# Three edits to an attention and convolution kernel: another queue for the last inverses, earlier reloads of the angle tables, and a new place for the sums of four heads

## The chip, the cores and the metric

The kernel runs on one core of one Trainium2 chip. A core has a matrix engine (TensorE, "PE" in the profile, with its weight loads listed apart as "PEld"), a vector engine (VectorE, "DVE"), an engine for activation functions (ScalarE, "ACT"), a general engine (GpSimd, "POOL") and one that only issues transfers (SyncE, "SP"). Each works through its own list of instructions in order and waits on semaphores for the others. Transfers are issued by SP or by POOL here, and all of them are carried out by the core's 16 DMA engines. The metric is the device time of one execution in microseconds.

## What is computed

Two layers are applied to a float32 input of shape (4, 1024, 32, 32), that is 4 images of 1024 channels and 1024 positions. The first layer is attention over the positions with 16 heads of 64 channels, the second is a bottleneck of three convolutions with normalization over the batch. Cut to what matters:

```python
# layer 1 of 2, per image: x is (N=1024 positions, C=1024 channels)
qkv = x @ w_qkv.T + b_qkv                 # q, k, v: 16 heads of 64
q, k = rope(q), rope(k)                   # pairs (2i, 2i+1) turned by cos and sin tables
q = q * rsqrt(mean(q * q) + eps) * q_w    # over all 1024 channels; k likewise
attn = softmax(q @ k.T / 8)               # per head
out = rmsnorm((attn @ v) @ w_proj.T) * norm_out_w + x
# layer 2 of 2
h = relu(bn(conv1x1(out)));  h = relu(bn(conv3x3(h)));  h = bn(conv1x1(h))
return relu(out + softplus(residual_scale) * h)
```

## The kernel before

The four images (the code calls them batches, b = 0 to 3) go through the attention layer one after the other; the convolutions follow. Channels lie on the 128 partitions, in eight tiles (NT = 8), and positions along the free axis in two halves of 512 (NCH = 2). For every image the stages are: projection to q, projection to k, projection to v, the scores and contexts of the heads, and the output projection.

**Projections.** They are matrix products by a Strassen-like scheme in two levels (`project2`; q and k of image 0 take one level, `project`). There are seven outer operand blocks k, with seven inner products each. One inner product of `project2` is a group of eight matmul instructions of 256 columns, since a float32 matmul is made of two. Each inner product needs a weight chunk of 256 KB, which SP loads into a ring of eight buffers (`chunk`); `start(k + 1)` queues the loads of the next block between the third and the fifth product of this one. Sums of weights were prepared in DRAM during image 0 (`wdf`, `wd2f`), by steps that share VectorE and SP with the attention of image 0. VectorE makes the sums of the right operands (L450 to L454) and adds partial results (L506, L525).

**The order of the work.** The lists of TensorE, POOL, VectorE and ScalarE are written out by hand, in the order in which the code emits; SP's list is ordered by the compiler's planner, which estimates times. The code keeps a clock of its own while it emits, `pace["at"]`, in units of one large product (two inner products of `project2` are one unit): `product_done` advances it, `after(n, step)` puts a step n units later, and `waiting` holds steps that go out when there is room on VectorE. While the last block of the v projection is emitted, `waiting` is held (`pace["hold"]`). `rest(leave)` empties the lists until `leave` steps remain.

**Rotation** (`rope`, L705 to L740). q and k are turned tile by tile: VectorE multiplies the tile by the sine table (into another buffer) and by the cosine table (in place), and POOL issues two accumulating transfers that add the first product with neighbouring rows exchanged (L727, "the exchange"). Before this, `tables` (L715) multiplies both tables in place by the inverse root mean square of this image. So the tables must be loaded anew before the next rotation: after the last tile POOL issues three loads (L176 twice for sines, L177 for cosines), and `then` holds the next rotation back until 3.7 units after the point at which the last tile was emitted.

**Scores and contexts** (`attention`). It is called for each half c of the query positions, and goes through eight pairs of heads (hp). For each of eight blocks t of key positions TensorE makes a score tile of both heads (`sc`, L787), ScalarE takes the exponential (L794), and VectorE adds it into the running denominators `d_` (L798 and L800). After the eight score tiles come the contexts (`cx`, L808). In the first half (c = 0) denominators are folded to eight heads at a time, by transfers of POOL (`halve`, `sum_of_eight`). In the second half (c = 1, `fold` is None), after each odd pair, four matmuls with a block of ones (`dn`, L841) sum the denominators of four heads over the partitions, directly behind the contexts. The three kinds of matmul use the array in different shapes: the records list them as 64*128 (scores), 128*64 (contexts) and 128*32 (denominators). At the start of the next pair ScalarE copies `dn` out (L891), SP stores it and loads it back in another layout, VectorE takes the reciprocal, and SP spreads the inverses over the partitions (`spread`, L910). `mean_of_v` then scales the contexts on VectorE (L764) and adds the bias of v on POOL (L765).

**The last four heads of an image** have no next pair. Their `dn` follows the last contexts, and their `inverses` step is emitted shortly after the start of the output projection: VectorE takes the reciprocal of all 512 columns (L893), SP stores them (L894) and spreads them by eight transfers (L910). `mean_of_v` for them is emitted three units after the start of the projection, and the sums of the second part of its right operands (L281 to L284) four units after. In the same stretch SP issues the weights of the projection and the loads of the next image (of the last: of what the convolution reads back, L1107).

Of the kernel before, what the change touches and what calls it, by code (L numbers as in the profile page):

```python
# [11 lines left out]
F32 = mybir.dt.float32  # L12
# [6 lines left out]
P = 128  # L19
B, C, H, W = 4, 1024, 32, 32  # L20
N = H * W
NT = C // P
HD = 64
NHP = C // (2 * HD)
CH = 512
# [38 lines left out]
QH = P // 4  # L64
# [21 lines left out]
def program(ctx, tc, x, wblk, w2, w3, vecs, cos, sin, out, bad):  # L86


    nc = tc.nc
# [9 lines left out]
    ones = const.tile([P, P], F32, name="ones")  # L99
# [16 lines left out]
    def col(name, i=0):  # L116
        return vec[:, COL[name] + i : COL[name] + i + 1]
# [35 lines left out]
    dens = dram.tile([P, CH], F32, name=f"dens{u}")  # L153
# [4 lines left out]
    with tc.tile_pool(name=f"st{u}", bufs=2) as st, ExitStack() as s:  # L158
# [6 lines left out]
        acc = s.enter_context(tc.tile_pool(name=f"acc{u}", bufs=2))  # L165
# [4 lines left out]
        cosT = tp.tile([P, N], F32, tag="cos", name="cosT")  # L170
        sinT = tp.tile([P, N], F32, tag="sin", name="sinT")

        def load_tables(queue):
            for i in range(2):

                queue.dma_start(sinT[i::2, :], sin[1 - i :: 2, :])  # L176
            queue.dma_start(cosT, cos)  # L177

        ident = None
# [5 lines left out]
        half = [slice(c * CH, (c + 1) * CH) for c in range(NCH)]  # L185
# [17 lines left out]
        def bank(kind, name):  # L203
            pool, shape = psum[kind]
            return pool.tile(shape, F32, tag=kind, name=name)
# [43 lines left out]
        pace = {"at": 0, "room": 0.0, "hold": False, "tables": 0.0}  # L249
# [459 lines left out]
        def rope(b, dst, total, eps, scale, w, tag, biased=True):  # L709

            def tables():
                for t in (sinT, cosT):
                    nc.vector.tensor_tensor(t, t, total, ALU.mult)  # L715

            def turn(f):
                k, other = dst[:, f, :], big_temp(f"{tag}s_{b}_{f}")
                for i, (t, table) in enumerate(((other, sinT), (k, cosT))):
                    if w is not None:  # L720
                        nc.vector.scalar_tensor_tensor(t, k, w[i][:, f : f + 1], table, ALU.mult, ALU.mult)
                    elif biased:
                        nc.vector.tensor_tensor(t, k, table, ALU.mult)
                    else:
                        nc.vector.scalar_tensor_tensor(t, k, col("bq", f), table, ALU.add, ALU.mult)
                for i in range(2):
                    nc.gpsimd.dma_start(dst[i::2, f, :], other[1 - i :: 2, :], accum_op=ALU.add)  # L727
                if f == NT - 1 and (b, tag) != (B - 1, "k"):
                    load_tables(nc.gpsimd)
                    pace["tables"] = pace["at"] + 3.7  # L730

            def then():
                if pace["at"] < pace["tables"]:
                    after(pace["tables"] - pace["at"], then)
                    return
                waiting.append((4 * TT, tables))
                for f in range(NT):
                    waiting.append((4 * TT, lambda f=f: turn(f)))

            inverse_rms(total, eps, scale, f"{tag}_{b}", then)  # L740
# [26 lines left out]
        def attention(b, c, q_all, k_all, v, probs_, late, ready, extra, slow, steps_in_all, load_parts, fold):  # L767


            at = half[c]  # L770
            sums_ = []
            for hp in range(NHP):
                n = f"{b}_{c}_{hp}"
                if late:
                    late.pop(0)()
                rows = shifts(q_all, k_all, n, hp, c) if bad is None else None
                probs = []
                if fold and hp % 2 == 0:
                    d_ = fold[hp // 4][:, hp % 4 // 2 * 2 : hp % 4 // 2 * 2 + 2, :]
                else:  # L780
                    d_ = acc.tile([P, 2, CH], F32, tag="tot", name=f"den_{n}")
                for t in range(N // P):
                    p = probs_[:, t]
                    sc = bank("sc", f"sc_{n}_{t}")
                    for j in range(2):
                        d = slice(j * HD, (j + 1) * HD)
                        nc.tensor.matmul(  # L787
                            sc[:, j], k_all[d, hp, t * P : (t + 1) * P], q_all[d, hp, at],
                            start=True, stop=bad is not None,
                        )  # L790
                    if bad is None:
                        for j in range(2):
                            nc.tensor.matmul(sc[:, j], ones[0:1, :], rows[j], start=False, stop=True)
                    nc.scalar.activation(p, sc, AF.Exp)  # L794
                    if t == 3:
                        load_parts()
                    if t == 1:
                        nc.vector.tensor_tensor(d_, probs[0], p, ALU.add)  # L798
                    elif t > 1:
                        nc.vector.tensor_tensor(d_, d_, p, ALU.add)  # L800
                    probs.append(p)
                if eights and eights[0][0] <= c * NHP + hp:
                    eights.pop(0)[1]()
                o = bank("cx", f"cx_{n}")
                for t in range(N // P):
                    for j in range(2):
                        h0 = (2 * hp + j) * HD
                        nc.tensor.matmul(  # L808
                            o[j * HD : (j + 1) * HD, :], v[:, t, h0 : h0 + HD], probs[t][:, j],
                            start=(t == 0), stop=(t == N // P - 1),  # L810
                        )

                nc.scalar.copy(q_all[:, hp, at], o)  # L813
                sums_.append(d_)
                if hp % 2 == 1:
                    for r in ready:
                        mean_of_v(q_all, *r)
                    ready.clear()
                if fold:
                    halve(hp, d_, fold[hp // 4][:, hp % 4 // 2 * 2 : hp % 4 // 2 * 2 + 2, :])  # L820
                    if hp % 4 == 3:
                        eights.append((hp + 2, lambda n=n, hp=hp: sum_of_eight(b, n, hp, fold[hp // 4], ready)))
                if half_done and half_done[0][0] <= c * NHP + hp:
                    half_done.pop(0)[1]()
                if slow:
                    slow.pop(0)()

                if waiting:
                    next_waiting()
                slots = NCH * NHP - 1  # L830
                if extra and steps_in_all == 0 and hp > 0:
                    extra.pop(0)()
                for _ in range(len(extra) - -(-steps_in_all * max(slots - 1 - c * NHP - hp, 0) // slots) if steps_in_all else 0):
                    extra.pop(0)()
                if hp % 2 == 0 or fold:
                    continue
                dn = bank("dn", f"dn_{n}")
                for i, d_ in enumerate(sums_):
                    for j in range(2):
                        q = slice((2 * i + j) * QH, (2 * i + j + 1) * QH)  # L840
                        nc.tensor.matmul(dn[q, :], ones[:, :QH], d_[:, j], start=True, stop=True)  # L841
                sums_ = []
                late.append(lambda *a, n=n, hp=hp, dn=dn: inverses(b, c, hp, n, dn, ready))

        half_done, eights = [], []
        low, high = slice(0, P // 2), slice(P // 2, P)
# [38 lines left out]
        def inverses(b, c, hp, n, dn, ready):  # L885


            r = temp(f"rec_{n}")
            k = 2 * ((b * NCH + c) * NHP + hp - 1)

            nc.scalar.copy(r, dn)  # L891
            if (c, hp) == (NCH - 1, NHP - 1):
                nc.vector.reciprocal(r, r)  # L893
                nc.sync.dma_start(dens[k : k + 4, :], r[::QH, :])  # L894
                spread(c, hp, n, ready, [r[q * QH : (q + 1) * QH, :] for q in range(4)])
                return
            few, rows = to_few(n, k, 4, r[::QH, :])

            def invert():
                nc.vector.reciprocal(few, few)  # L900
                nc.sync.dma_start(rows, few)
                spread(c, hp, n, ready, [dens[k + q, :].partition_broadcast(QH) for q in range(4)])

            half_done.append((0, invert))

        def spread(c, hp, n, ready, rows):
            w = big_temp(f"inv_{n}")
            for i in range(2):
                for j in range(4):
                    nc.sync.dma_start(w[j * QH : (j + 1) * QH, half[i]], rows[2 * i + j // 2])  # L910
                ready.append((c, hp - 1 + i, w[:, half[i]]))

        def o_norm(b, total, ys):
# [245 lines left out]
        load_x(0, 0, range(NH, NT))  # L1159
        w1 += [block(WQ, g, 1, f"q_0_{g}_1") for g in range(NG)]  # L1160
        load_x(0, 1)
        load_tables(nc.sync)
        queue_sums(ts[0], xs[0])
        room = v_room("rq_0")
        for b in range(B):
# [500 lines left out]
```

## Time and profile before

| | |
|---|---|
| median of 3 runs | 2677.93 us (2675.83 to 2679.2) |
| profiled execution | 2679.37 us, its span on the core 2677.6 us |
| granted TensorE clock, mean | 0.997 |
| VectorE busy | 2112.0 us (79%) |
| ScalarE busy | 1113.8 us (42%) |
| POOL busy | 434.3 us (16%) |
| DMA queue of SP (hardware) | 328.75 MB, 39.3% of 16 engines' span |
| DMA queue of POOL (software) | 131.45 MB, 20.7% |
| scores and contexts, image 0 / 1 / 2 / 3 begin at | 287.8 / 864.6 / 1442.1 / 2017.7 us |
| output projection, image 0 / 1 / 2 / 3 begins at | 522.4 / 1096 / 1674 / 2249.4 us |

The page gives the busy time of each engine and, for each group of instructions, what ended the idle time before it. A wait that is put down to one engine ended with that engine's instruction. The timeline lists instructions by start and length in microseconds from the start of the span, merges neighbours of one kind (x16 means sixteen), and writes in brackets the idle time of the engine before and who ended it. An "SPq" line is an issue: the transfer itself lands later.

### The profile page before, as it was taken

The page shows a single profiled execution, that of the slowest core. Times are in us where ns is not written, and L with a number is a line of the kernel's source. Part 1 is how long each engine was busy: PE and PEld are TensorE (multiplying, and loading weights), DVE is VectorE, ACT ScalarE, POOL GpSimd, SP SyncE. Part 2 cuts the span into 40 slices and gives each one's busy share as a digit, 9 for nine tenths or more (in the row PEclk, how much of TensorE's full clock was granted, in tenths as well). Part 3 has the DMA queues.
Part 4 walks back from the last instruction along what each step waited for, and adds up shares of the span by engine and source line. Part 5 has one row for each costly group of instructions (what it writes and reads, how often), then busy time and mean ns, then how long its engine had stood idle before and what let it go on. Part 6 is the DMA issues. An engine that isn't in the chain of part 4 may idle for free. (4 is left out here: it accounts for less than half of the span.)

```text
span 2677.6 us, 32431 instructions
## 1 busy us (share of the span) xinstructions
PE 2646.0 (99%) x11322; PEld 1652.9 (62%) x11322; DVE 2112.0 (79%) x2536; ACT 1113.8 (42%) x1551; POOL 434.3 (16%) x501
## 2 busy tenths in 40 slices
PE   9999999999999999999999999999999999999997
PEld 4448533488888333688886333888884335846843
DVE  5668989997888766888878767887978679877987
ACT  2222455423442555333343555233525554312266
POOL 2542202100111222100111222100111222010000
PEclk9999999999999999999999999999999999999999
DMA  7887787767667551556775441665774443593165
GB/s 279 289 253 216 223 239 239 239 201 221 201 186 204 96 92 34 166 156 218 194 199 131 92 79 30 213 204 175 192 212 87 80 103 105 163 279 115 64 232 208
DMA packets 261387, 462.37 MB, mean 173 GB/s; under 512 B 34528, under 2 KB 127248, under 8 KB 261216
## 3 DMA queue, kind: packets, MB, share of 16 engines
q1 hardware_dynamic: 222048, 328.75, 39.3%
q0 software_dynamic: 39168, 131.45, 20.7%
q8 instruction: 93, 1.52, 0.2%
q14 instruction: 78, 0.64, 0.1%
HBM read 327.43 MB, written 97.01 MB: 159 GB/s over the span
## 5 line engine op out<-in xcount | busy, mean ns | idle before, releaser
L794 ACT ACTIVATE p<-sc 128x1024 f32<-128x1024 f32 x512 | 476.7, 1047 | 26.5 <-PE sc L787 25.8
L787 PE MATMUL sc<-q,k 64*128 64x512 f32 x2048 | 457.7, 596 | 0.0
L800 DVE TENSOR_TENSOR den<-den,p 128x1024 f32<-128x1024 f32 x288 | 356.1, 1236 | 30.4 <-DVE den L800 0.5
L787 PEld LDWEIGHTS sc<-q,k 64*128 64x128 f32 x2048 | 189.9, 186 | 265.2 <-issue 121.7
L808 PE MATMUL cx<-p,to 128*64 128x512 f32 x1536 | 340.2, 595 | 0.0
L808 PEld LDWEIGHTS cx<-p,to 128*64 128x64 f32 x1536 | 106.0, 137 | 228.8 <-issue 228.8
L480 PE MATMUL p_v<-w_v,x 128*128 128x256 f32 x928 | 211.7, 382 | 2.8 <-DVE x L451 2.8
L485 PE MATMUL p_y<-q,w_y 128*128 128x256 f32 x928 | 209.8, 379 | 0.0
L765 POOL TENSOR_SCALAR q<-q,vec 128x512 f32<-128x512 f32 x64 | 128.2, 2014 | 436.3 <-DVE q L764 436.3
L480 PEld LDWEIGHTS p_v<-w_v,x 128*128 128x128 f32 x928 | 177.3, 191 | 28.6 <-DVE x L451 3.9
L485 PEld LDWEIGHTS p_y<-q,w_y 128*128 128x128 f32 x928 | 176.0, 190 | 27.1 <-issue 3.4
L813 ACT COPY q<-cx 128x512 f32<-128x512 f32 x64 | 37.6, 587 | 360.7 <-PE cx L808 360.7
L798 DVE TENSOR_TENSOR den<-p 128x1024 f32<-128x1024 f32 x48 | 59.7, 1245 | 117.5 <-ACT p L794 117.5
L485 PE MATMUL p_q<-to,w_q 128*128 128x256 f32 x672 | 152.2, 379 | 0.0
L485 PE MATMUL p_k<-to,w_k 128*128 128x256 f32 x672 | 152.2, 379 | 0.0
L485 PEld LDWEIGHTS p_q<-to,w_q 128*128 128x128 f32 x672 | 127.4, 190 | 18.4 <-issue 1.2
L485 PEld LDWEIGHTS p_k<-to,w_k 128*128 128x128 f32 x672 | 127.4, 190 | 18.4 <-issue 1.2
L800 DVE TENSOR_TENSOR den_T<-den_T,p 128x1024 f32<-128x1024 f32 x96 | 117.6, 1226 | 10.4 <-ACT p L794 0.5
L808 PE MATMUL cx<-p,rq 128*64 128x512 f32 x512 | 113.4, 595 | 0.0
L1570 PE MATMUL c<-h,w 128*128 128x512 f32 x256 | 110.3, 592 | 0.5 <-ACT h L1473 0.5
L485 PE MATMUL p_y<-to,w_y 128*128 128x256 f32 x384 | 91.3, 383 | 5.8 <-DMA w_y<-wdf 5.8
L480 PE MATMUL p_v<-w_v,t 128*128 128x256 f32 x384 | 90.2, 379 | 0.9 <-DMA w_v<-wdf 0.8
(488 smaller groups left out, 4205.0 us busy)
## 6 DMA issues: line engine op xcount, KB each, us to landing
w_v<-wd2f SPq DMA_DIRECT2D x112, 256.0 KB, 3.3
w_y<-wd2f SPq DMA_DIRECT2D x112, 256.0 KB, 2.8
w_q<-wd2f SPq DMA_DIRECT2D x84, 256.0 KB, 2.7
w_k<-wd2f SPq DMA_DIRECT2D x84, 256.0 KB, 2.7
wd2f<-w_pre SPq DMA_DIRECT2D x68, 256.0 KB, 2.7
x<-in_x_dram SPq DMA_DIRECT2D x64, 256.0 KB, 5.0
q<-qs POOLq DMA_DIRECT2D x64, 256.0 KB, 5.5
k<-ks POOLq DMA_DIRECT2D x64, 256.0 KB, 4.4
```

Source lines behind the costliest of these rows:

```text
L480: nc.tensor.matmul(o[:, q].rearrange("p (g f) -> p g f", g=2), r[:, i, q * P : (q + 1) * P], wt[:, :, i, :], skip_group_check=True, **at,)
L485: nc.tensor.matmul(o[:, q], wt[:, q, i, :], r[:, i, :], skip_group_check=True, **at)
L765: nc.gpsimd.tensor_scalar(cx, cx, col("bv", hp), None, ALU.add)
L787: nc.tensor.matmul(sc[:, j], k_all[d, hp, t * P : (t + 1) * P], q_all[d, hp, at], start=True, stop=bad is not None,)
L794: nc.scalar.activation(p, sc, AF.Exp)
L798: nc.vector.tensor_tensor(d_, probs[0], p, ALU.add)
L800: nc.vector.tensor_tensor(d_, d_, p, ALU.add)
L808: nc.tensor.matmul(o[j * HD : (j + 1) * HD, :], v[:, t, h0 : h0 + HD], probs[t][:, j], start=(t == 0), stop=(t == N // P - 1),)
L813: nc.scalar.copy(q_all[:, hp, at], o)
L1570: nc.tensor.matmul(os[i], w3t[k][f // NH][:, f % NH, :], h2[b, k][:, half[c]], start=(k == 0), stop=(k == NPT - 1),)
```

## The change

It has three parts. First, `load_tables` is split into the sines and the cosines, and each is issued right behind the product that used the old table of the last tile, ahead of that tile's two exchange transfers; the next rotation is held back 5 units instead of 3.7. Second, in the second half of the attention the four `dn` matmuls of a group are no longer emitted behind the contexts of the odd pair, but in the next pair behind its second score tile, together with the copy and the store that follow them; the running denominators of that next pair get their buffer after this. The last group of an image stays where it was. Third, for this last group the store and the eight spreads are issued by POOL's queue instead of SP's.

```diff
-        def load_tables(queue):
+        def load_sines(queue):
             for i in range(2):
                 queue.dma_start(sinT[i::2, :], sin[1 - i :: 2, :])
+
+        def load_cosines(queue):
             queue.dma_start(cosT, cos)
...
                         nc.vector.scalar_tensor_tensor(t, k, col("bq", f), table, ALU.add, ALU.mult)
+                    if f == NT - 1 and (b, tag) != (B - 1, "k"):
+                        (load_sines, load_cosines)[i](nc.gpsimd)
                 for i in range(2):
                     nc.gpsimd.dma_start(dst[i::2, f, :], other[1 - i :: 2, :], accum_op=ALU.add)
-                if f == NT - 1 and (b, tag) != (B - 1, "k"):
-                    load_tables(nc.gpsimd)
-                    pace["tables"] = pace["at"] + 3.7
+                if f == NT - 1:
+                    pace["tables"] = pace["at"] + 5
...
-            sums_ = []
+            sums_, fours = [], []
...
-                if fold and hp % 2 == 0:
-                    d_ = fold[hp // 4][:, hp % 4 // 2 * 2 : hp % 4 // 2 * 2 + 2, :]
-                else:
-                    d_ = acc.tile([P, 2, CH], F32, tag="tot", name=f"den_{n}")
+                d_ = None
...
                     if t == 1:
+                        if fours:
+                            fours.pop()()
+                        if fold and hp % 2 == 0:
+                            d_ = fold[hp // 4][:, hp % 4 // 2 * 2 : hp % 4 // 2 * 2 + 2, :]
+                        else:
+                            d_ = acc.tile([P, 2, CH], F32, tag="tot", name=f"den_{n}")
                         nc.vector.tensor_tensor(d_, probs[0], p, ALU.add)
...
-                dn = bank("dn", f"dn_{n}")
-                for i, d_ in enumerate(sums_):
-                    for j in range(2):
-                        q = slice((2 * i + j) * QH, (2 * i + j + 1) * QH)
-                        nc.tensor.matmul(dn[q, :], ones[:, :QH], d_[:, j], start=True, stop=True)
+
+                def sum_of_four(n=n, hp=hp, sums_=sums_):
+                    dn = bank("dn", f"dn_{n}")
+                    for i, d_ in enumerate(sums_):
+                        for j in range(2):
+                            q = slice((2 * i + j) * QH, (2 * i + j + 1) * QH)
+                            nc.tensor.matmul(dn[q, :], ones[:, :QH], d_[:, j], start=True, stop=True)
+                    return lambda: inverses(b, c, hp, n, dn, ready)
+
                 sums_ = []
-                late.append(lambda *a, n=n, hp=hp, dn=dn: inverses(b, c, hp, n, dn, ready))
+                if hp < NHP - 1:
+                    fours.append(lambda f=sum_of_four: f()())
+                else:
+                    late.append(sum_of_four())
...
                 nc.vector.reciprocal(r, r)
-                nc.sync.dma_start(dens[k : k + 4, :], r[::QH, :])
-                spread(c, hp, n, ready, [r[q * QH : (q + 1) * QH, :] for q in range(4)])
+                nc.gpsimd.dma_start(dens[k : k + 4, :], r[::QH, :])
+                spread(c, hp, n, ready, [r[q * QH : (q + 1) * QH, :] for q in range(4)], nc.gpsimd)
                 return
...
-        def spread(c, hp, n, ready, rows):
+        def spread(c, hp, n, ready, rows, queue=nc.sync):
...
-                    nc.sync.dma_start(w[j * QH : (j + 1) * QH, half[i]], rows[2 * i + j // 2])
+                    queue.dma_start(w[j * QH : (j + 1) * QH, half[i]], rows[2 * i + j // 2])
...
-        load_tables(nc.sync)
+        load_sines(nc.sync)
+        load_cosines(nc.sync)
```

## The prediction

> **What bounds the kernel now.** I read the page's busy times, then TensorE's waits, then three stretches of the timeline.
>
> ```profile
> PE 2646.0 (99%) x11322; PEld 1652.9 (62%) x11322; DVE 2112.0 (79%) x2536; ACT 1113.8 (42%) x1551; POOL 434.3 (16%) x501
> ```
>
> TensorE is busy for 2646.0 of 2677.6 us, so whatever does not move a matmul is worth nothing. Its waits, from the list of waits of that engine:
>
> ```profile
> PE p_y L485 <- DMA w_y<-wdf: 5.8, 4, 2.3
> PE p_v L480 <- DVE x L451: 2.8, 2, 2.0
> PE dn L841 <- DVE den L800: 0.3, 1, 0.3
> ```
>
> These are three of the places that the change touches. The lists count open gaps only; the timeline shows what a stall costs in all. TensorE at the start of the last batch's projection:
>
> ```profile
> 2263.32 5.34 PE L485 MATMUL p_y<-y,w_y 128*128 128x256 f32 x24
> 2270.95 2.84 PE L485 MATMUL p_y<-to,w_y 128*128 128x256 f32 x8 [2.29 <-DMA w_y<-wdf]
> 2273.59 2.77 PE L485 MATMUL p_y<-y,w_y 128*128 128x256 f32 x8
> 2276.20 1.89 PE L485 MATMUL p_y<-to,w_y 128*128 128x256 f32 x8
> ```
>
> SP's queue in the same stretch says why:
>
> ```profile
> 2255.92 0.51 SPq L894 DMA_DIRECT2D densf<-rec  x1
> 2256.47 4.99 SPq L910 DMA_DIRECT2D inv<-rec  x8
> 2261.57 2.22 SPq L472 DMA_DIRECT2D w_y<-wd2f  x4
> 2263.89 0.40 SPq L383 DMA_DIRECT2D w_y<-in_wblk_dram  x1
> 2264.37 0.93 SPq L383 DMA_DIRECT2D w_y<-wdf  x2
> ```
>
> SP stood at L894 from 2252.8 for VectorE's 3.35 us reciprocal, then issued nine DMAs until 2261.5. Behind them stood the weights of operand block k=1, whose ring buffers had been coming free since about 2253. They went out in a bunch, and the first weight of block k=2, last in the bunch, needed 6.5 us from 2264.37 to the matmul at 2270.95; the tile view of w_y has a median landing of 2.8.
>
> The third place is the value projection of batch 2; POOL's queue, then VectorE's:
>
> ```profile
> 1393.75 1.67 POOL L727 DMA_DIRECT2D q<-qs  x2 [10.58 <-issue]
> 1394.85 1.67 POOL L176 DMA_DIRECT2D sinT<-in_sin_dram  x2
> 1395.96 1.09 POOL L177 DMA_DIRECT2D cosT<-in_cos_dram  x1
> ```
>
> ```profile
> 1402.79 1.23 DVE L715 TENSOR_TENSOR sinT<-sinT,sqk 128x1024 f32<-128x1024 f32 x1 [6.51 <-DMA sinT<-in_sin_dram]
> 1404.75 1.23 DVE L715 TENSOR_TENSOR cosT<-cosT,sqk 128x1024 f32<-128x1024 f32 x1 [0.74 <-DMA cosT<-in_cos_dram]
> 1406.61 0.69 DVE L451 TENSOR_TENSOR x<-t,x 128x512 f32<-128x512 f32 x1
> ```
>
> VectorE waits in order for reloaded tables, and the sums that TensorE needs (L451) stand behind.
>
> Last, the denominators' matmuls, in the weight loads of TensorE:
>
> ```profile
> 459.70 0.14 PEld L808 LDWEIGHTS cx<-p,rq 128*64 128x64 f32 x2 [0.28 <-issue]
> 460.66 0.16 PEld L841 LDWEIGHTS dn<-den,ones 128*32 128x32 f32 x8 [0.81 <-DVE q L764]
> 461.66 0.30 PEld L787 LDWEIGHTS sc<-q,k 64*128 64x128 f32 x4 [0.84 <-issue]
> 468.72 0.20 PEld L808 LDWEIGHTS cx<-p,rq 128*64 128x64 f32 x4 [0.76 <-issue]
> 475.74 0.30 PEld L787 LDWEIGHTS sc<-q,k 64*128 64x128 f32 x4 [0.81 <-issue]
> ```
>
> A phase of scores takes 7.07 us, one of contexts 7.02, an unstalled dn 1.00. The steady step inside is 0.43 for two loads, so 16 steps are 6.88: each phase of scores carries 0.19 us for the change of array shape.
>
> **What the Trainium skill says.** "TensorEngine Tiling (Array Packing)", Key Properties: a change of the tiling mode drains the engine. The trace agrees: the last load before a change stands 0.94 to 0.96 us before the next, where 0.43 is usual. "TensorE: Matmul & The Clock Gate", What's actually happening: an array that has idled through a window of about 3.4 us runs at half clock until it has been busy again. The trace agrees in part: after the stalls at 2270.95 and 1407.36 matmuls come at half pace for some microseconds, and here little over 2 us of standing was enough; after the shorter ones they don't. "DMA: Bandwidth & Descriptors", Issuing engines are not separate DMA queues: DMAs of all engines share the same 16 DMA engines, so another queue saves the issuing only. Here it is the issuing that blocks.
>
> **Part 1, inverses by POOL's queue.** One store (0.51 us) and eight spreads (4.99) a batch leave SP with their wait; k=1's weights then go out one by one as buffers come free, and k=2's first, issued near 2264.4, lands 2.8 later, at 2267.2, before its turn at 2268.5. What the stalls cost, by starts of matmuls at the steady 0.216 us: batch 0, due 536.28+24x0.216=541.46, came 542.58: 1.1; batch 1, 1116.15 for 1115.15: 1.0; batch 2, 1694.64 for 1692.79: 1.85; batch 3, 2270.95 for 2268.50: 2.45, and the next two groups took 2.64 and 2.61 instead of 1.73: 1.8 more. With 0.1 in each first group after the shorter three: 8.5 us.
>
> What POOL pays: its queue is free (its last work, L765, ends at 2252.7). Its issues follow each other at 0.55 us (L176 to L177), so with a start 0.5 after the reciprocal's end at 2255.9 the ninth leaves at 2260.8. POOL's copies of den (L854, L855) land after 3.5 us in the median: the last inverse is there at 2264.3, where SP's was at 2262.9 (its landings are 2.0). The two POOL additions (L765) stand behind, 4.0 us. VectorE asks for the first half at 2263.62 (there from about 2262.1) and for the second at 2264.22: at most a few tenths late. VectorE is in order, so sums L281 to L284 and the sums of block 2 follow. Their slack: L282 ends at 2269.75, and unstalled TensorE wants it for its second product of block 2 at 2271.95: 2.2 us. Cost nothing; if all landings were 8 us (the longest of those copies), the last would come at 2268.8, L282 would end near 2272.6 and TensorE would lose some 1 to 2 us a batch.
>
> **Part 2, tables ahead of the exchange, and a later use.** Sines go out once the product with them is done, cosines after the other product; the two exchanges of the last tile (1.1 us of POOL) fall behind, and nobody wants them before the scores, 40 us on. In batch 2 VectorE's last read of sines ends at 1390.6, and sines now go out near 1392 instead of 1394.9, cosines near 1393 instead of 1396.0. With today's 6.7 to 8.8 us from issue to landing the sines are there by 1399.5, the cosines by 1402. The use falls later too: the due time counts in half units of 1.73 us, so 3.7 acts as 4.0, and 5 puts it two products, 3.5 us, on, behind the sums L450 to L454 that TensorE waits for now. Both gains go one way, and I take all of the stall: batch 2 had 1407.36 for 1405.18, 2.2, and 23 matmuls in 6.92 for 5.13, 1.8; batch 3 1984.67 for 1983.67, 1.0; batch 1 0.1: 5.1 us. The turns of k that follow come 3.5 later, two before the scores as now (they ran at 1409.6 and 1418.1, scores begin at 1442.1); if the second slips to the start of the scores it costs VectorE 2.5 us there, and VectorE is busy 105 of 143 us in that stretch, so TensorE doesn't see it. In batch 0 tables were used at 225.6, long after landing at 189: nothing.
>
> **Part 3, sums of four behind the second score tile.** Twelve groups (three in each batch) move; the last of each batch stays. Each breaks a phase of scores in two and so adds one shape change: 0.19. The dn itself costs its 1.00 as now. The copy of dn falls on ScalarE between the exponentials of tiles 1 and 2, where it fills a gap: tile 2 comes 1.2 us later. The sum of tile 1 waits for dn, since it writes a buffer that dn reads, and both come at about 3 us: nothing. In batches 1 to 3 no dn waits today (all 1.00), so 9x0.19=1.7 is lost. In batch 0 dn took 1.73, 2.00 and 2.36 for 1.00. Two of these move away from their stall (1.7), but VectorE has no free microsecond between 476 and 522, and the last dn, unmoved, waits for its end at 521.3. What TensorE gains it waits there: nothing, at best 1.7.
>
> **Sum.** -8.5-5.1+1.7=-11.9 us on the profiled execution's 2679.37 (span 2677.6 and 1.8 around it), 2667.5. The median of the runs is 2677.93, 1.4 lower, so 2666.0 in terms of runs; I leave 0.5 for small waits: 2666.5. A measurement here can tell about 0.2%, 5.4 us, from no change.
>
> **Rivals.**
> A (70%): as summed; 2663.5 to 2671.
> B (16%): the weights are late anyway, or the inverses. For it: in batch 0 the DMA engines are busy 86% between 520 and 545, x loads compete, and SP's order is a planner's, which may fill the hole with x loads. Against: 73% to 76% in the other batches. Then only part 2 less part 3 is left: -3.4, 2674.5.
> C (8%): tables are still late, as they share the DMA engines with the weights, and part 1 holds: -8.5+1.7=-6.8, 2671.
> D (6%), the slower side: the turns of k. During the last block of the value projection the queue of waiting steps is held. If the delayed tables push the first turn from 1409.6 past the start of that hold, about 1432, it comes at the first score, which needs it: 2.5 of VectorE, 0.6 to issue, 4.4 landing (tile view of k), about 7.5 us in each of three batches and 1.8 of half clock: +28. With part 1's 8.5 and part 2's 5.1 gone and part 3's 1.7: 2677.9+28-11.9=2694. It decides from a delay of 22 us; I see 3.5.
> Faster by over 0.2%: nearly all of A and most of C, 0.75; within: B and their edges, 0.17; slower 0.08. Range 2662 (batch 0's 1.7 and a little more gained) to 2676 (B and 1.5).
>
> **What would show it.** Right: no wait of p_y on w_y from wdf and none of p_v on L451; SP goes from x loads to L472 without a pause; 36 issues of inv and dens on POOL at 0.55; dn within the scores, with 7.26 plus 1.00 for the split phase; batch 0's last dn waits longer than 1.36. Wrong: a wait of VectorE at L764 over 2.2 us, k turns inside the scores' first 8 us in threes, or a dn that waits between scores in batches 1 to 3.

## The result and the profile after

| | before | after |
|---|---|---|
| median of 20 runs | 2673.72 us (2672.0 to 2679.2) | 2679.6 us (2672.78 to 2683.88) |
| ratio after to before | | 1.0018 [1.0011, 1.0025] |
| profiled execution | 2679.37 us, span 2677.6 | 2682.08 us, span 2680.3 |

The changed kernel is slower by 0.18%, 4.8 us by the ratio, where 11.9 us were to be gained. That lies within the 0.2% that the forecast called no change, though the interval stays above 1; the forecast's range, 2662 to 2676 us, doesn't hold the time. The profiled execution of before lies above all of its 20 runs, 5.7 us over their median, and that of after 2.5 us over its own, so what one profile shows is a sample. The forecast's base, a median of three runs (2677.93), lay 4.2 us over the median of 20.

The page's busy times of after:

```profile
PE 2647.8 (99%) x11322; PEld 1653.9 (62%) x11322; DVE 2111.6 (79%) x2536; ACT 1113.1 (42%) x1551; POOL 453.0 (17%) x537
```

POOL has 36 instructions more: four stores and 32 spreads. In the waits of TensorE in after (total us, times, longest), the wait for the tables is gone, and the wait for the weights of block k=2, which was to go, has grown from 5.8 to 10.0:

```profile
PE p_y L487 <- DMA w_y<-wdf: 10.0, 4, 3.2
...
PE dn L850 <- DVE den L807: 0.4, 1, 0.4
```

Where each stage gained or lost is told by its length: from TensorE's first matmul of the stage to its first of the next, in us, summed over the images (worked out from the starts in each trace). The unstalled lengths come from experiments told of below: 84.7 for one output projection, 85.47 for one value projection.

```
                                    before   after   unstalled
output projection, images 0 to 3    347.4    354.9   338.8
value projection, images 1 to 3     261.6    256.4   256.4
attention, images 1 to 3            694.8    696.4
attention, image 0                  234.6    233.5
```

The second row is part 2 of the change, the third part 3, and the first part 1: most of the loss is there, 7.5 us in these two profiles (a second profile of after, told of below, had 348.3 in this row). TensorE in after, in the stretch of image 3 that the prediction opened with:

```profile
2266.74 5.34 PE L487 MATMUL p_y<-y,w_y 128*128 128x256 f32 x24
2275.31 1.99 PE L487 MATMUL p_y<-to,w_y 128*128 128x256 f32 x8 [3.22 <-DMA w_y<-wdf]
2277.14 1.89 PE L487 MATMUL p_y<-y,w_y 128*128 128x256 f32 x8
```

It stands 3.22 us where it stood 2.29. SP's queue in after, for the same place of image 1:

```profile
1100.51 1.42 SPq L217 DMA_DIRECT2D x<-in_x_dram  x3
1102.02 0.38 SPq L474 DMA_DIRECT2D w_y<-wd2f  x1
1102.44 0.43 SPq L217 DMA_DIRECT2D x<-in_x_dram  x1
1103.54 0.33 SPq L474 DMA_DIRECT2D w_y<-wd2f  x1
1103.91 0.43 SPq L217 DMA_DIRECT2D x<-in_x_dram  x1
...
1109.14 1.18 SPq L217 DMA_DIRECT2D x<-in_x_dram  x2
1110.44 0.39 SPq L385 DMA_DIRECT2D w_y<-wdf  x1
```

SP is never blocked, and the weights of k=1 (L474) go out one by one, as forecast. But between them stand loads of the next image (L217), 256 KB each, in the place that the spreads left. TensorE at the end of that stretch:

```profile
1111.98 5.34 PE L487 MATMUL p_y<-y,w_y 128*128 128x256 f32 x24
1119.71 3.55 PE L487 MATMUL p_y<-to,w_y 128*128 128x256 f32 x8 [2.39 <-DMA w_y<-wdf]
```

The first weight of k=2 was issued at 1110.44 and its matmul ran at 1119.71, 9.3 us later; it was due at 1111.98 + 24x0.216 = 1117.16. The DMA view says why. First before, 1102 to 1118, then after, 1104 to 1120 (busy share of the 16 engines in 40 slices, and what each queue moved, in packets, MB and share of the 16 engines' time):

```profile
DMA  9899655616336155154699989594589999999999
...
q1 hardware_dynamic: 2560, 3.78, 74.6%
```

```profile
DMA  9899989999978999999999989999999999999999
...
q1 hardware_dynamic: 2901, 4.60, 90.1%
q0 software_dynamic: 288, 0.53, 11.5%
```

Before, the DMA engines stand half idle while SP is blocked. After, there is little slack in them: SP's queue moves 0.8 MB more, though the spreads have left it, and the 0.53 MB of the spreads come by POOL's queue.

### The profile page after: what moved, and what is told of

Its sections match the earlier page's. It is cut to its first block, busy times and chain, and to the rows that moved or that the text cites. A ratio compares the mean times of both kernels' runs of the same rounds, so it can differ in the third digit from the quotient of the medians.

```text
span 2680.3 us, 32478 instructions
## 1 busy us (share of the span) xinstructions
PE 2647.8 (99%) x11322; PEld 1653.9 (62%) x11322; DVE 2111.6 (79%) x2536; ACT 1113.1 (42%) x1551; POOL 453.0 (17%) x537
## 4 chain that ended last, share of the span: by engine, by line
PE 92%; DMA 4%; DVE 3%; ACT 1%; issue 0%; SPq 0%; POOL 0%; DVEq 0%; ACTq 0%
PE sc L788 16%; PE cx L815 15%; PE p_v L482 13%; PE p_y L487 11%; PE p_k L487 9%; PE p_q L487 9%; PE c L1587 4%; PE pa_q L305 2%; PE c2x L1438 2%; PE c L1006 2%; PE c2y L1438 2%; PE pa_k L305 1%; DMA w_y<-wdf 1%; PE c L965 1%; PE pc_q L305 1%; DMA x<-in_x_dram 1%
## 5 line engine op out<-in xcount | busy, mean ns | idle before, releaser
L807 DVE TENSOR_TENSOR den<-den,p 128x1024 f32<-128x1024 f32 x288 | 354.9, 1232 | 33.6 <-ACT p L795 4.4
L482 PE MATMUL p_v<-w_v,t 128*128 128x256 f32 x384 | 90.1, 379 | 0.0
```

The costliest lines, as they stand in the source:

```text
L482: nc.tensor.matmul(o[:, q].rearrange("p (g f) -> p g f", g=2), r[:, i, q * P : (q + 1) * P], wt[:, :, i, :], skip_group_check=True, **at,)
```

## The experiments

Four theories were put up on the loss. T1: the hole in SP's queue is filled with loads of the next image, and these are too much for the DMA engines. T2: the transfers on POOL's software queue take turns from the weights. T3: the inverses land late by POOL's queue, VectorE waits for them in order, and the sums that TensorE needs stand behind. T4, formed after the first four runs, joins the first two: weights and image loads alone just fit into the DMA engines, and what POOL's queue moves on top makes the weights late. Times are medians; ratios are to the kernel before on the same chip.

**Part 2 alone** on the kernel before (`load_sines`, `load_cosines` and the due time 5, nothing else):

> The kernel before with part 2 alone (tables ahead of the exchange, next rotation held 5 units). Value projections of images 1 to 3 at 85.5 each (85.6, 89.4 and 86.6 in the profile of the kernel before), output projections as in the kernel before (347.4 in sum), attention as in the kernel before. By the profile 5 us faster than the kernel before; if the waits for tables in that profile were longer than usual, less, 2 to 4. If SP's order shifts with it, output projections differ from the kernel before although nothing in them was edited.

Measured: 2670.93 us (21 runs), ratio 0.9985 [0.9979, 0.9992], so 4 us. The output projections, in which nothing was edited, took 342.8 us in this profile, a little less than in any of three profiles of before (343.7 to 347.4); whether part 2 has a share in that isn't known. The value projections of images 1 to 3 take 256.4 us, as in every run that has part 2.

**Part 1 undone** in after:

```diff
-                nc.gpsimd.dma_start(dens[k : k + 4, :], r[::QH, :])
-                spread(c, hp, n, ready, [...], nc.gpsimd)
+                nc.sync.dma_start(dens[k : k + 4, :], r[::QH, :])
+                spread(c, hp, n, ready, [...])
```

> The changed kernel with part 1 undone: the last inverses are stored and spread by SP's queue again; tables and sums of four stay changed. Theory 1 (the hole that part 1 leaves on SP's queue is filled with loads of the next image, and these and the weights together are more than the DMA engines can move in time), theory 2 (transfers from POOL's software queue take turns on the DMA engines away from the weights) and theory 3 (the inverses come late and hold VectorE) all say that the output projections go back to the lengths of the kernel before: 85.9, 85.8, 86.7 and 89.0 us, 347.4 in sum instead of 354.9; the value projections stay at 85.5. Some 7.5 us faster than the changed kernel, 2672. If the sum stays above 352, part 1 is not the cause at all and the order that part 3 gives SP is.

Measured: 2673.1 us (13 runs), ratio 0.9991 [0.9983, 1.0]. After has 1.0018 [1.0011, 1.0025]: part 1 costs 0.27%, 7.2 us, beside parts 2 and 3. The output projections take 343.6 us in this profile; the two of after had 354.9 and 348.3.

**The spreads left out.** The eight spreads of an image's last group are not issued, and these contexts are scaled by a constant instead; SP's queue stays as in after:

```diff
+            if queue is nc.gpsimd:
+                nc.gpsimd.memset(w, 1e-3)
...
-                for j in range(4):
+                for j in range(4 if queue is nc.sync else 0):
```

> The changed kernel with the eight spreads of the last four heads of each image left out (POOL fills the tile with a constant instead, so the last contexts are scaled wrongly); the store of the sums stays on POOL's queue, SP's queue stays free. Theory 1: SP still sends the next image's loads ahead of the weights, so the wait for w_y stays at 2 to 3 us in each image and the sum of the output projections at 352 to 355, 2679. Theory 2: the 8 x 64 KB of POOL are gone, the wait goes, sum near 343. Theory 3: no late inverses, the wait goes, sum near 343.

Measured: 2667.18 us (6 runs), ratio 0.9967 [0.9955, 0.9979]; each output projection takes 84.71 us. The DMA view of this kernel from 1101 to 1117, columns as above, and TensorE there:

```profile
DMA  8899689999999999999979899899999999999979
...
q1 hardware_dynamic: 3389, 5.48, 98.7%
```

```profile
1109.46 5.34 PE L487 MATMUL p_y<-y,w_y 128*128 128x256 f32 x24
1114.64 1.89 PE L487 MATMUL p_y<-to,w_y 128*128 128x256 f32 x8
```

The DMA engines are as full as in after and SP's loads stand between the weights as there, yet block 2 begins on time. So the image loads by themselves (T1) are not enough. This run can't tell T2 from T3, as both go with the spreads.

It does show what the spreads take from the DMA engines. Until 10 us after the start of the projection SP's queue has moved as much in both kernels (2.98 MB in the 12 us up to then); then the spreads come. The next 8 us, first in after (1108.06 to 1116.06), then here (1105.55 to 1113.55):

```profile
q1 hardware_dynamic: 1145, 1.85, 80.5%
q0 software_dynamic: 288, 0.53, 23.1%
```

```profile
DMA packets 1882, 2.76 MB, mean 345 GB/s; under 512 B 196, under 2 KB 887, under 8 KB 1881
q1 hardware_dynamic: 1849, 2.74, 99.5%
```

POOL's 0.53 MB push out 0.89 MB of SP's, and the engines move less in all, 2.39 MB for 2.76. At 345 GB/s 0.89 MB are 2.6 us, and block 2 came 2.55 us late in after (1119.71 for 1117.16). Whether this is due to POOL's queue or to the size of the spreads' pieces isn't settled: no run sent them by a third hardware queue.

**The next image's loads on ScalarE's queue**, all three parts kept. There each load stands behind the copies and exponentials of that queue, and can't run ahead:

```diff
-        def load_x(b, c, rows=range(NT)):
+        def load_x(b, c, rows=range(NT), queue=nc.sync):
...
-                            load_x(b + 1, c, (i,))
+                            load_x(b + 1, c, (i,), nc.scalar)
...
-                    after(5 + 1.5 * j, lambda i=i: read_back(1, (i,)))
+                    after(5 + 1.5 * j, lambda i=i: read_back(1, (i,), nc.scalar))
```

> The changed kernel with the loads of the next image (and, at the last image, the read-back) issued by ScalarE's queue, whose order is written by hand: two loads each 1.5 units, paced by the copies of the projection. POOL keeps the spreads, SP keeps only the weights. Theory 1: the loads no longer run ahead of the weights of block 2, the wait for w_y goes, output projections near 85.5 to 86 each, 343 in sum, 12 us faster than the changed kernel, 2668. Theory 2: the spreads still come through POOL's queue, so the wait stays, sum over 350. Theory 3: VectorE still waits over 3 us at the scaling of the last contexts, sum over 350. The loads cost ScalarE 0.4 to 0.5 us each; if that delays its copies, small waits of TensorE for PSUM appear instead.

Measured: 2667.04 us (6 runs), ratio 0.997 [0.9958, 0.9982], each output projection 84.71 us. POOL's transfers are all there and do no harm. So T2 by itself falls too: the stall needs both the image loads among the weights and POOL's spreads. That is T4. T3 is not excluded by these two, since with the image loads out of the way the spreads land earlier.

**The inverses sent, but not used.** Everything is transferred as in after; the product at L768 multiplies the last group's contexts by themselves, so VectorE waits for no inverse:

```diff
-            nc.vector.tensor_tensor(cx, cx, w, ALU.mult)
+            nc.vector.tensor_tensor(cx, cx, cx if w is None else w, ALU.mult)
...
-                ready.append((c, hp - 1 + i, w[:, half[i]]))
+                ready.append((c, hp - 1 + i, w[:, half[i]] if queue is nc.sync else None))
```

> The changed kernel with every transfer as it is, but the last contexts of each image are multiplied by themselves instead of by the spread inverses (so that part of the computation is left out and nothing waits for the inverses). SP's order is the same as in the changed kernel. Theory 3 (late inverses hold VectorE and so TensorE): the waits go, output projections 84.7 each as in the two runs without a stall, 2667. Theory 4, formed from the runs with the loads on ScalarE and without spreads (the engines are full with weights and image loads, and POOL's 0.5 MB on top are the part that makes the weights late): the wait for w_y stays at 2 to 3 us in each image, output projections 88 to 89, 2678 to 2680.

First VectorE in after, at the two products with the last inverses of image 1:

```profile
1113.64 0.69 DVE L768 TENSOR_TENSOR q<-q,inv 128x512 f32<-128x512 f32 x1 [1.28 <-DMA inv<-rec]
1116.45 0.69 DVE L768 TENSOR_TENSOR q<-q,inv 128x512 f32<-128x512 f32 x1 [2.12 <-DMA inv<-rec]
```

It does wait, 16.5 us in eight waits over the run, 3.7 at the longest: over the 2.2 us that the prediction named as a sign of being wrong. Then the waits of TensorE in the kernel that doesn't wait for inverses:

```profile
PE p_y L487 <- DMA w_y<-wdf: 7.0, 4, 2.4
```

The weights are still late. Measured: 2677.32 us (21 runs), ratio 1.001 [1.0003, 1.0016]; the output projections take 348.6 us, as in the second profile of after. Most of the loss stays: T3 may hold some 2 us (ratio 1.001 for 1.0018), and as the intervals of the two ratios overlap, even these aren't certain.

**Part 1 alone** on the kernel before:

> The kernel before with part 1 alone. Theory 4: SP's hole fills with image loads as in the changed kernel, the engines are over 0.9 busy in the first 23 us of each output projection, the projections take 88 to 89 each (355 in sum), while the value projections keep their waits for tables: 6 to 9 us slower than the kernel before, 2681 to 2684. If part 1 only does harm together with the others, within 3 us of the kernel before.

Measured: 2677.29 us (13 runs), ratio 1.001 [1.0001, 1.0018]: a loss of 2.7 us, hardly clear of noise, where T4 as written expected 6 to 9. So the 0.27% is shown beside parts 2 and 3 only, and why it is smaller here was not followed up. The profile caught the fastest of the 13 runs (2672.72): the weights of block 2 are late in every image, 7.3 us in all, and the output projections take 347.2 us, 86.3 to 87.6 each for the expected 88 to 89. The value projections took 257.2 us, with the tables loaded as before: that stall differs from run to run.

**Part 2 and the paced image loads, spreads left on SP:** the kernel before, with `load_sines`, `load_cosines`, due time 5, and `nc.scalar` for the image loads.

> Part 2 and the image loads on ScalarE's queue, with the inverses spread by SP as before. SP stands for the reciprocal, the weights of block 1 go out in a bunch, but nothing of the next image stands among or before them. Theory 4: the bunch of 8 weights is 2 MB, 6 to 7 us at 300 to 340 GB/s, so the first weight of block 2 is at the edge: 0 to 1 us of wait in each image, output projections 84.7 to 85.7, 2665 to 2669. If a blocked SP queue alone makes the stall, 1 to 2 us in each image, as in the kernel before, 2669 to 2672.

Measured: 2672.98 us (13 runs), ratio 0.9992 [0.9983, 1.0], output projections 343.4 us. SP's queue in this kernel in image 1, and then TensorE:

```profile
1102.76 5.00 SPq L914 DMA_DIRECT2D inv<-rec  x8
1107.86 1.52 SPq L474 DMA_DIRECT2D w_y<-wd2f  x3
...
1110.40 0.88 SPq L385 DMA_DIRECT2D w_y<-wdf  x2
```

```profile
1116.15 1.99 PE L487 MATMUL p_y<-to,w_y 128*128 128x256 f32 x8 [0.97 <-DMA w_y<-wdf]
```

No image load is near on SP's queue (ScalarE's brings 1.03 MB of them between 1102 and 1118), and block 2 still waits 0.97 us. A blocked SP queue makes a stall without image loads in it: 343.4 less 338.8, 4.6 us in four images. The time lies above both expectations, 2669 and 2672 at most. Pacing the image loads alone brings nothing (0.9985 without it, 0.9992 with it).

**Parts 1 and 2 with the paced image loads, without part 3:** the edit just told of, and the store and spreads on `nc.gpsimd`.

> Parts 1 and 2 without part 3, and the image loads on ScalarE's queue. Output projections 84.7 each, value projections 85.5, and each of images 1 to 3 without the three extra shape changes in its attention: 231.4 instead of 232.04. 1.5 to 2 us faster than the changed kernel with the loads on ScalarE (2667.0), so 2665 to 2665.5. If part 3 is worth more in image 0 than it costs in the others, equal or slower: 2667 to 2668.

Measured: 2665.16 us (6 runs, 2664.92 to 2666.68), ratio 0.9965 [0.9953, 0.9977], output projections 338.8 us. This is the lowest median of all and below both kernels; the interval of the kernel with part 3 on top (0.997) overlaps with it. SP's queue in image 1, the DMA view from 1102 to 1118, and TensorE:

```profile
1098.38 5.50 SPq L474 DMA_DIRECT2D w_y<-wd2f  x4
1105.29 0.38 SPq L385 DMA_DIRECT2D w_y<-in_wblk_dram  x1
1107.01 2.09 SPq L385 DMA_DIRECT2D w_y<-wdf  x2
```

```profile
DMA  3095959589665699989999997399999979744965
...
q1 hardware_dynamic: 1649, 2.31, 50.9%
q10 hardware_dynamic: 604, 1.11, 20.9%
q0 software_dynamic: 288, 0.53, 10.6%
```

```profile
1108.55 5.34 PE L487 MATMUL p_y<-y,w_y 128*128 128x256 f32 x24
1113.73 1.89 PE L487 MATMUL p_y<-to,w_y 128*128 128x256 f32 x8
```

SP issues weights alone, waits for its ring buffers only, and q10, ScalarE's queue, brings the image in between. The engines have gaps again, and block 2 begins in step: 1108.55 + 24x0.216 = 1113.73.

The runs make a table that shows part 1's sign turn with the place of the image loads (ratios; all have part 2, the upper row has part 3 as well, the lower one not, and part 1 with neither gave +0.001):

```
                              spreads by SP   spreads by POOL   part 1
image loads on SP             0.9991          1.0018            +0.0027
image loads on ScalarE        0.9992          0.9965            -0.0027
```

**Scatter of the profiles.** The two kernels unedited, one more profile of after and two of before:

> The changed kernel, unedited, profiled once more. Theory 4 expects the wait for w_y of 1.5 to 4 us in each output projection again, 350 to 355 in sum, and value projections of images 1 to 3 at 85.47 as in every run with part 2.

> The kernel before, unedited, profiled once more. Its first profile (2679.37) lies above nearly all later runs of it (median 2675.3), and the kernel with part 1 alone, which has the old tables, lost only 1.1 us in its value projections where that profile lost 5.1. If the first profile was an unlucky one, this one shows waits for tables of 1 to 3 us in sum and output projections of 344 to 346. If it was a usual one, 4 to 5 us and 347.

> The kernel before, unedited, a third profile, for the spread of the waits: the same expectation as for the second.

Measured, as what the output projections take over 338.8 us: before 8.6 in the first profile, then 4.9 and 8.3; after 16.1, then 9.5. What the value projections take over 256.4: before 5.2, then 3.5 and 4.0; after 0 both times. The 348.3 us of the second profile of after lie below the 350 to 355 that T4 expected. So the stalls of one profile are a sample, and those that the forecast was summed from were the largest of three.

## Why the prediction was wrong, step by step

**Part 1, forecast -8.5, measured +7.2 (after against part 1 undone).** The step that failed is "k=1's weights then go out one by one as buffers come free, and k=2's first, issued near 2264.4, lands 2.8 later, at 2267.2, before its turn at 2268.5". Its first half came true. The landing did not: with the issue at 2265.21 in image 3, the matmul ran at 2275.31, 10.1 us later, and 9.3 us in image 1. The 2.8 us were the median over loads into w_y, in a run whose two large queues filled 60% of the engines' span in the mean (39.3 and 20.7); the term was not priced for the stretch in which it was to hold. The blocked SP queue had held back the image loads too, and so had kept the DMA engines free for what came behind it; unblocked, it sends both. That the blocked queue does delay the weights was right (the spreads on SP without image loads still stall, by 4.6 us in all), and so was the worth of the stall: with the image loads paced the output projections fall from 347.4 to 338.8, 8.6 us for the forecast 8.5. That the two agree so closely is luck: the other two profiles of before had 4.9 and 8.3 to gain.

The Trainium skill was cited for this, "DMA: Bandwidth & Descriptors", Issuing engines are not separate DMA queues: all share the 16 DMA engines. The text concluded that "Here it is the issuing that blocks" and left the sharing out of the sum. These runs agree with the page: with the spreads under way SP's queue moved 1.85 MB in 8 us, without them 2.74. Per MB, POOL's queue took 21.7% of the 16 us window (11.5 by 0.53) and SP's 19.6% (90.1 by 4.60), for 18.0% without the spreads (98.7 by 5.48).

**The price of POOL's queue, forecast "Cost nothing".** Also wrong, in a smaller term. The issues come every 0.50 us (0.55 was taken), but the spreads land after 6.3 us in the median, not 3.5, and 8.9 at the longest; with the image loads paced it is 3.3 (and 3.2 with part 3). The bound given for landings of 8 us, 1 to 2 us an image, lies above what was found: the run without the wait gives at most some 2 us in four images, not clear of noise. The larger price, that the spreads take the DMA engines from the weights, was not in the sum at all.

**Part 2, forecast -5.1: right.** The stall is gone in every run, -5.2 in the two profiles and about -4 in the runs of part 2 alone. POOL and then VectorE in after, image 2:

```profile
1396.17 1.12 POOL L176 DMA_DIRECT2D sinT<-in_sin_dram  x2 [6.35 <-DVE qs L727]
1397.49 0.55 POOL L179 DMA_DIRECT2D cosT<-in_cos_dram  x1 [0.20 <-issue]
1398.03 1.79 POOL L732 DMA_DIRECT2D q<-qs  x2
```

```profile
1401.81 1.23 DVE L717 TENSOR_TENSOR sinT<-sinT,sqk 128x1024 f32<-128x1024 f32 x1 [0.29 <-DMA sinT<-in_sin_dram]
1404.67 1.23 DVE L717 TENSOR_TENSOR cosT<-cosT,sqk 128x1024 f32<-128x1024 f32 x1 [1.63 <-DMA cosT<-in_cos_dram]
1405.81 0.68 DVE L452 TENSOR_TENSOR x<-t 128x512 f32<-128x512 f32 x1
```

The loads go out ahead of the exchanges, 0.3 us after the product with the old sines ends (4.2 before), and VectorE waits 1.9 us for them instead of 7.3. One half of the reason was not seen: the use did not move behind the sums, L452 still follows it. The earlier issue was enough here; the later due time was not tried alone.

**Part 3, forecast +1.7: right.** Weight loads of TensorE in after, where a group's sums now break a phase of scores:

```profile
1616.61 0.19 PEld L788 LDWEIGHTS sc<-q,k 64*128 64x128 f32 x2 [0.23 <-issue]
1617.56 0.16 PEld L850 LDWEIGHTS dn<-den,ones 128*32 128x32 f32 x8 [0.76 <-DVE few L916]
1618.56 0.30 PEld L788 LDWEIGHTS sc<-q,k 64*128 64x128 f32 x4 [0.84 <-issue]
```

The phase begins at 1615.64 and its contexts at 1623.91: 8.27 us, less 1.00 for `dn` 7.27, where 7.26 was forecast. Images 1 to 3 lose 0.59, 0.41 and 0.59 us. In the runs with paced image loads the kernel with part 3 takes 2667.04 and that without 2665.16, 1.9 us, though by the ratios (0.997 and 0.9965) it is 1.3 and their intervals overlap; it is the profiles' 1.6 us that are clear. In image 0 the attention took from 233.5 to 235.4 us in three profiles of before and 233.4 to 233.5 in two of after: too much scatter for a gain of 1.7 to be seen or denied. The last `dn` of image 0 was to wait longer than 1.36 us; it waited 0.4.

**The sum.** From the runs: part 1 +7.2, part 2 -4, part 3 +1.9 make +5.1, and +4.8 was measured. Part 1 was measured as the last step up to the changed kernel, so only part 3's number is an independent one in this sum. Once image loads don't fill the hole, the change takes 2667.04, close to the forecast 2666.5, but this too is luck in part: the gain is 0.3%, 8 us, for the 11.4 forecast in terms of runs, and the forecast's base was 4.2 us high.

**The rivals.** B had the mechanism, "SP's order is a planner's, which may fill the hole with x loads", with 16%, but was priced as a gain that fails to come, 2674.5; that the loads could make the weights later than they had been was left out. Its counter-argument, engines busy 73% to 76%, was a mean that included the hole itself. C and D did not come.

## What to carry to other kernels

A queue that stands blocked also holds back everything else behind it, and that can be what keeps the DMA engines free for the transfer that matters: before moving a wait off a queue, list what will run ahead in its place and add those bytes to the stretch, not to the mean. Free the queue and pace the other loads together; each alone brought nothing or a loss here. A landing time is a price only for the load that it was measured under.

## What the runs showed of the hardware that was not expected

- A software-queue transfer of 64 KB landed after 3.2 to 3.3 us in the median where the DMA engines had gaps (the two kernels with paced image loads and part 1) and after 6.3 us where they were full (after).
- A second queue can cost full DMA engines more than its bytes: in the 8 us in which the spreads run, in all images of the four profiles in which POOL sends them and SP the image loads, SP's queue moved 1.80 to 2.04 MB, and 2.65 to 3.08 in the kernel without the spreads, for the 0.47 to 0.53 MB that POOL's queue brought.
- The scatter of a kernel goes with its late weights, not with full DMA engines as such: 20 runs of after spread over 11.1 us and 13 of the kernel with SP's spreads and paced image loads over 8.5, while the three kernels whose output projections don't stall spread over 1.8 to 2.3 us (six runs each; the first six of the other two spread over 8.0 and 5.1), the one with engines at 98.7% among them.
- Half-pace matmuls do not follow from the length of a stall, but from how it falls on a grid of time. The stall of 2.39 us before 1119.71 and the one of 3.22 us before 2275.31 in after, in windows of this grid (the number behind the first comma is how long TensorE was busy, PEclk the granted clock):

```profile
core 0: us, PE busy (x) PEld busy (x) DVE busy (x) ACT busy (x) POOL busy (x), PEclk, DMA share, GB/s
1116.57:1119.98 3.41, 1.02 (x5) 0.59 (x4) 2.31 (x3) 0.59 (x1) 2.66 (x1) 1.00 1.07 374
1119.99:1123.40 3.41, 3.41 (x9) 2.68 (x9) 3.14 (x3) 0.10 (x1) 0.24 (x1) 0.50 0.63 232
2270.28:2273.69 3.41, 1.81 (x9) 1.25 (x7) 0.91 (x2) 1.17 (x2) 0.60 (x2) 1.00 1.06 350
2273.70:2277.11 3.41, 1.80 (x8) 1.62 (x9) 2.03 (x3) 0.00 (x0) 2.85 (x1) 1.00 0.89 332
2277.12:2280.52 3.40, 3.40 (x17) 2.99 (x16) 3.40 (x4) 1.17 (x2) 0.00 (x0) 1.00 0.45 111
```

  The first stall lies in one window, 2.39 of its 3.41 us, and the next window runs at half clock; the longer one is split, 1.60 and 1.61, and nothing follows. In the clock records of all 13 profiles, between 12 and 2640 us, the clock changes only on such a grid. Half clock came seven times, for one window each, and TensorE had stood for 1.86 to 2.39 us of the window before; in no other window had it stood for more than 1.79. "TensorE: Matmul & The Clock Gate" in the Trainium skill (What's actually happening) names a free-running idle window of about 3.4 us: length and free running agree with these records, but the window need not be idle throughout, 1.86 of 3.41 us were enough. What the activity limit is beyond this bracket of 1.79 to 1.86 the runs don't show.
- So much of the scatter is where a stall happens to fall. The two profiles of after stood 10.0 and 8.4 us for weights; the first had three windows of half clock, the second none, and at some 1.7 us each (half of 3.41) these make 5.1 of the 6.6 us between their output projections. The 1.8 us of half pace that the prediction counted in image 3 of before came in two of its three profiles: in the other a stall of 2.30 us was split 0.60 and 1.70.
